# Drawing one layernorm at a time beside quantisation, and the first layernorm on VectorE, in a six-stage transformer kernel

## The chip, the cores and the metric

The kernel runs on one NeuronCore of a Trainium2 chip. The metric is device microseconds of one execution. TensorE is called PE here, VectorE DVE, ScalarE ACT, GpSimd POOL and SyncE SP, as the profile writes them.

## The reference

Sequence length 2048, width 256, 16 heads, hidden width 1024. Two kinds of feed-forward, two kinds of attention, a layernorm in front of each:

```python
x = x + 0.5 * ffn0(layernorm(x))     # stage f0: ternary-quantised weights, silu gate, rms norm
x = x + attn0(layernorm(x))          # ALiBi, causal
x = x + 0.5 * ffn0(layernorm(x))     # stage f1
x = x + 0.5 * ffn1(layernorm(x))     # stage f2: silu gate, 2:4 sparsified
x = x + attn1(layernorm(x))          # RoPE, causal
x = x + 0.5 * ffn1(layernorm(x))     # stage f3

def layernorm(x): return (x - mean(x)) / sqrt(var(x) + 1e-5)
def ternary_quant(w):                # groups of 64, in bf16
    scale = clip(mean(abs(w_g)), 1e-8); q = clip(round(w_g / scale), -1, 1); return q * scale
def ffn0(x): h = silu(x @ Wg) * (x @ Wu); return rms_norm(h) @ Wp
```

## The kernel before

Activations lie transposed: features on the 128 partitions (two halves of 256, `dc`), tokens along the free dimension, in four chunks of 512 tokens (`c` = 0 to 3). `xs[c]` holds the residual, `xns[c]` the normalised input of the next step; both are fp32 tiles of 128x2x512. The order of instructions on PE, ACT, DVE and POOL is that of the program text (a manual schedule), so Python generators decide it: each generator issues a few instructions and yields.

**A layernorm** (`layernorm(c, name)`, L244 to L278) is such a generator with about six steps. Step 1: POOL adds the two feature halves (`s`, L252). After two yields: PE sums over partitions with a matrix of 1/256 (`pm`, L256), DVE subtracts the mean (`xc`, L258), ACT squares (L261), POOL adds the halves of the squares (`v`, L263). Two yields later: PE sums `v` (`pv`, L269), `root` transposes on DVE (`tt`, L208, a single buffer) and takes the square root on ACT (L210, for which ACT loads another activation table, and a second one to go back to silu). Last step: `spread` (reciprocal L215, transpose L217 into `sd`), then two POOL products write `xn` (L274).

**Quantisation** (`quantize(i)`, L129) turns the fp32 weights of stage f0 and f1 into twelve tiles of 128x512 bf16: tiles 0 to 7 into `wgu0` (gate and up), 8 to 11 into `wp0` (down). Each has two ACT operations (L150, L152), one matmul into the single `acc` bank (`psq`, L155) and a set of six DVE operations (L158 `sc`, L162 `big`, L165 `df`, L167 `q`, L169 `wh`, L170 result). `quants` holds the generator of all of them until it is through; four sets are issued beside the first layernorm, the other eight during chunk 0 of stage f0.

**Stage f0** goes over the four chunks in order. A chunk has eight gate/up steps (`f` = 0 to 7): twelve matmuls into a pair of banks (`pg`, L311, two pairs in all, with the input as three bf16 parts), silu on ACT (`sl`, L322), product on DVE (`h`, L323), two DVE operations that split `h` into bf16 parts (`hm` L339, last part L334), and a square on ACT and a sum on POOL for the rms norm (`sq` L344, `ss` L345). At `f` = 6 or 7 the next chunk's input is split (`xm`, `xn`: L240, L241, only if its layernorm is fully issued). The tail of the chunk before (`tail0`: 24 matmuls `po` L361 for each feature half, `pss`, `tt_rms`, `y` L372, the residual update on POOL L373) is issued at `f` = 0 to 3 of the chunk after it.

What is issued beside each step comes from the deque `background`, which first holds the layernorms of chunks 1 to 3; when a chunk's tail is through, the layernorm in front of the attention (`after_f0_c`) is put behind them. `pull()` (L193) advances the first two generators of `background` by one step each; it is called once in every `f` step, right after the step's own instructions. From `f` = 4 of chunk 2 on, `go_on` also issues the start of the attention: a memset, then the key projection of chunk 0 (`pp_k`, L561, four fp32 matmul passes on `xns[0]`).

So the loop order around the change is: `f` step, quantisation, `pull()`, tail step, quantisation, split, attention start.

Of the kernel before, what the change touches and what calls it, by code (L numbers as in the profile page):

```python
# [15 lines left out]
ALU = mybir.AluOpType  # L16
# [3 lines left out]
P = 128  # L20
S = 2048
E = 256
DC = E // P
# [6 lines left out]
CH = 512  # L30
# [16 lines left out]
def macaron_kernel(ctx: ExitStack, tc: tile.TileContext, a, out):  # L47
    nc = tc.nc
# [12 lines left out]
    def ps_one(name):  # L61
        return ps3.tile([P, CH], F32, tag="one", name=name)
# [19 lines left out]
    def load_x(c, engine):  # L82
        engine.dma_start(
            out=xs[c], in_=a["xT"][:, c * CH : (c + 1) * CH].rearrange("(dc p) s -> p dc s", p=P)
        )
# [97 lines left out]
    background = deque()  # L183
# [8 lines left out]

    def pull():  # L193

        for work in list(background)[:2]:
            if next(work, "end") == "end":
                background.remove(work)

    def ready(c):

        while pending[c]:
            pull()

    def root(ps, eps, scale, name):


        tt = lpool.tile([P, CH // SLOT, SLOT], F32, tag="tt", name=f"tt_{name}")
        nc.vector.transpose(tt.rearrange("p b s -> p (b s)"), ps)  # L208
        r = lpool.tile([P, CH // SLOT], F32, tag="r", bufs=3, name=f"r_{name}")
        nc.scalar.activation(r, tt[:, :, 0], AF.Sqrt, bias=eps, scale=scale)  # L210
        return r

    def spread(r, pool, bufs, name):

        nc.vector.reciprocal(r, r)  # L215
        sd = pool.tile([P, CH], F32, tag="sd", bufs=bufs, name=f"sd_{name}")
        nc.vector.transpose(  # L217
            sd.rearrange("p (b s) -> p b s", s=SLOT),
            r.unsqueeze(2).to_broadcast([P, CH // SLOT, SLOT]),
        )  # L220
        return sd
# [19 lines left out]
        nc.vector.tensor_tensor(low(xn), mid, high(mid), ALU.subtract)  # L241
        return high(xn), high(mid), low(xn)

    def layernorm(c, name, slack=0):  # L244

        pending[c] += 1
        asked.add(name)

        def pieces():
            x, xn = xs[c], xns[c]  # L250
            s = lpool.tile([P, CH], F32, tag="s", bufs=2, name=f"s_{name}")
            nc.gpsimd.tensor_tensor(s, x[:, 0, :], x[:, 1, :], ALU.add)  # L252
            for _ in range(2 + slack):
                yield
            pm = ps_one(f"pm_{name}")
            nc.tensor.matmul(pm, lhsT=mean_m, rhs=s, start=True, stop=True)  # L256
            xc = lpool.tile([P, DC, CH], F32, tag="xc", bufs=2, name=f"xc_{name}")
            nc.vector.tensor_tensor(  # L258
                xc, x, pm.unsqueeze(1).to_broadcast([P, DC, CH]), ALU.subtract
            )  # L260
            nc.scalar.activation(xn, xc, AF.Square)  # L261
            v = lpool.tile([P, CH], F32, tag="s", bufs=2, name=f"v_{name}")
            nc.gpsimd.tensor_tensor(v, xn[:, 0, :], xn[:, 1, :], ALU.add)  # L263
            yield
            yield
            while gate[0]:
                yield
            pv = ps_one(f"pv_{name}")
            nc.tensor.matmul(pv, lhsT=mean_m, rhs=v, start=True, stop=True)  # L269
            r = root(pv, eps_ln, 1.0, f"ln_{name}")  # L270
            yield
            sd = spread(r, lpool, 2, f"ln_{name}")
            for dc in range(DC):
                nc.gpsimd.tensor_tensor(xn[:, dc, :], xc[:, dc, :], sd, ALU.mult)  # L274
            pending[c] -= 1
            yield

        return pieces()  # L278


# [181 lines left out]
    def feed_forwards(stages, beside, own=None):  # L462


        with tc.tile_pool(name=f"ffn_{stages[0][1]}", bufs=1) as hp:
# [4 lines left out]
            for s, (kind, stage, order) in enumerate(stages):  # L470
                for at, c in enumerate(order):
# [8 lines left out]
                    for f in range(FC):  # L480
                        next(work)
                        quantize_on()
                        pull()
                        if tail and f in tail[0]:
                            next(tail[1])
                            if f == tail[0][-1]:
                                tail[2]()
                                tail = None
                        draw(sparse)
                        quantize_on()  # L490
                        if kind == 0 and f >= FC - 2 and not xp and at + 1 < NCH:
                            b = order[at + 1]
                            if not pending[b]:
                                xp = split(b, own, f"{stage}_{b}")
                        beside(s, at, f)

                    def done(c=c, s=s):
                        if s == len(stages) - 1:
                            ending(c, stages[s][1])
                        else:  # L500
                            background.append(layernorm(c, f"{stages[s + 1][1]}_{c}", 1))
# [15 lines left out]
    def attention(layer, before, following):  # L517
# [9 lines left out]
        with ExitStack() as st:  # L527
# [321 lines left out]
            def output(c, dc):  # L849
                po = ps_one(f"pwo{layer}_{c}_{dc}")  # L850
                for q in range(G // 2):
                    nc.tensor.matmul(  # L852
                        po,
                        lhsT=wo[:, q, dc * P : (dc + 1) * P],
                        rhs=zs[c][:, q, :],
                        start=q == 0,
                        stop=q == G // 2 - 1,
                    )
                if layer == 0:
                    nc.vector.tensor_tensor(xs[c][:, dc, :], po, xs[c][:, dc, :], ALU.add)  # L860
                else:
                    nc.vector.scalar_tensor_tensor(
                        xs[c][:, dc, :], po, b_o[:, dc : dc + 1], xs[c][:, dc, :], ALU.add, ALU.add
                    )
                if dc == DC - 1:
                    (background if c == 0 else held).append(
                        layernorm(c, f"{following}_{c}")
                    )
# [120 lines left out]
            for i, (n, kb) in enumerate(slots):  # L989
# [40 lines left out]
                if preps and (c <= 1 or i % 2):  # L1030
                    step()
                    if c == 0 and i % 2:
                        draw(background)
                else:
                    pull()
# [8 lines left out]
    def ending(c, stage):  # L1044

        if stage == "f3":
            nc.sync.dma_start(
                out=out[:, c * CH : (c + 1) * CH].rearrange("(dc p) s -> p dc s", p=P), in_=xs[c]
            )
        else:  # L1050
            background.append(layernorm(c, f"after_{stage}_{c}", 1))

    def quantizer():

        tiles = [quantize(i) for i in range(6 * DC)]
        for i in range(3):
            next(tiles[i])
        for i, q in enumerate(tiles):
            next(q)
            if i + 3 < len(tiles):  # L1060
                next(tiles[i + 3])
            yield
            next(q)
            yield

    quants = [quantizer()]
# [37 lines left out]
        begun.clear()  # L1104

    load_x(0, nc.scalar)
    ln = layernorm(0, "f0_0")
    for k in range(6):
        next(ln)
        if k in (0, 2, 4, 5):  # L1110
# [121 lines left out]
```

## Time and profile before

| what | value |
|---|---|
| three runs | 1888.13, 1891.71, 1891.57 us; median 1891.57 |
| the profiled execution's own time | 1893.92 us |
| its span, first to last instruction | 1892.1 us, mean granted PE clock 0.973 |
| busy share of the span | PE 91%, DVE 72%, ACT 46%, POOL 21% |
| chain that ended last | PE 68%, DVE 23%, ACT 4% of the span |
| stage f0 | about 5 to 240 us of the span; its chunks begin with the first `pg` at 21, 79, 123 and 168 us |

Times in the profile are microseconds from the span's start. A row of the timeline gives start, duration, engine, line, operation, output and inputs, and in brackets the idle time of that engine before it and what ended it. A row "x2" merges two instructions in a row.

### The profile page before, as it was taken

To read this page: it belongs to the slowest core of one execution; us is meant where nothing else is said; L and a number is where in the kernel's file an instruction comes from. 1 tells how busy PE (TensorE), PEld (TensorE's weight loads), DVE (VectorE), ACT (ScalarE), POOL (GpSimd) and SP (SyncE) were. 2 spreads that over 40 slices of the span, in tenths; PEclk is the share of its full clock that TensorE was granted. 3 is DMA by queue.
4 is the path that set the end of the run, shared out by engine and by line. 5 is a ranking of instruction groups with operands and counts; after the bars stand their busy time and mean duration, and the time that the engine had idled before them with its cause. 6 is when DMAs were issued, how large, how long until landed. Compare 5 with 4: busy or idle time off the path is not lost.

```text
span 1892.1 us, 27018 instructions
## 1 busy us (share of the span) xinstructions
PE 1728.9 (91%) x10658; PEld 743.1 (39%) x10684; DVE 1359.6 (72%) x2400; ACT 878.0 (46%) x1148; POOL 406.6 (21%) x386
## 2 busy tenths in 40 slices
PE   5689988999999999798999998889999999989999
PEld 1234443433434443333434344434334344433443
DVE  7867577787788884577666667878887888816665
ACT  4234353555556667433332233445555656673221
POOL 3345620100000001345422342211011000013100
PEclk9799999999999999999999998999999999999999
DMA  4002332222211010200000134323122111000000
GB/s 133 2 1 68 111 110 66 77 56 72 89 55 47 29 29 2 75 1 0 1 12 0 39 106 128 93 80 99 53 59 85 61 36 35 11 2 0 12 12 23
DMA packets 50511, 93.11 MB, mean 49 GB/s; under 512 B 5424, under 2 KB 33072, under 8 KB 50128
## 3 DMA queue, kind: packets, MB, share of 16 engines
q1 hardware_dynamic: 49296, 89.28, 15.6%
q10 hardware_dynamic: 1088, 2.10, 0.3%
q8 instruction: 84, 1.38, 0.3%
q14 instruction: 43, 0.35, 0.1%
HBM read 59.51 MB, written 27.26 MB: 46 GB/s over the span
## 4 chain that ended last, share of the span: by engine, by line
PE 68%; DVE 23%; ACT 4%; issue 2%; POOL 1%; DMA 1%; SPq 0%; DVEq 0%; ACTq 0%; POOLq 0%
PE pav L811 14%; PE pst L776 12%; PE pq L714 11%; DVE mx L725 7%; PE pg_f L286 7%; PE pg_f L311 5%; PE po_f L297 5%; PE po_f L361 4%; PE pv L626 2%; PE pwo L852 2%; PE pp_k L561 2%; DVE h_f L334 1%; PE pp_q L561 1%; DVE hm_f L339 1%; DVE ge_f L413 1%
## 5 line engine op out<-in xcount | busy, mean ns | idle before, releaser
L725 DVE TENSOR_REDUCE mx<-pq 128x1 f32<-128x512 f32 (+3 forms) x1280 | 696.6, 601 | 137.2 <-PE pq L714 68.4
L796 ACT ACTIVATE pT<-pst 128x1024 f32<-128x1024 f32 (+3 forms) x616 | 536.0, 896 | 339.6 <-PE pst L776 177.0
L714 PE MATMUL pq<-k,q 105*128 105x512 bf16 (+7 forms) x1280 | 388.9, 353 | 49.6 <-DVE mx L725 43.6
L776 PE MATMUL pst<-q,k 99*128 99x512 bf16 (+7 forms) x1280 | 359.5, 355 | 10.5 <-ACT pT L796 6.7
L811 PE MATMUL pav<-pT,va 128*32 128x256 f32 (+1 forms) x4608 | 326.0, 379 | 6.2 <-DVE yt L832 5.0
L286 PE MATMUL pg_f<-xn,wgu 128*128 128x512 f32 x512 | 233.4, 608 | 12.5 <-DVE hr_f L323 12.5
L837 POOL TENSOR_TENSOR zt<-yt,rd 128x64 f32<-128x64 f32 x128 | 42.0, 328 | 807.6 <-DVE rd L836 807.6
L776 PEld LDWEIGHTS <-k 105*128 105x128 bf16 (+1 forms) x1280 | 111.6, 98 | 234.5 <-issue 170.2
L811 PEld LDWEIGHTS pav<-pT,va 128*32 128x32 f32 x4608 | 106.4, 109 | 189.9 <-issue 135.2
L714 PEld LDWEIGHTS <-q 105*128 105x128 bf16 (+1 forms) x1280 | 124.2, 99 | 131.9 <-issue 31.4
L311 PE MATMUL pg_f<-xn,wgu 128*128 128x512 bf16 x500 | 150.7, 406 | 20.0 <-DVE wgu L170 6.8
L322 ACT ACTIVATE sl_f<-pg_f 128x512 f32<-128x512 f32 x128 | 75.6, 591 | 190.4 <-PE pg_f L286 101.9
L286 PEld LDWEIGHTS pg_f<-xn,wgu 128*128 128x128 f32 x512 | 98.4, 194 | 143.4 <-issue 116.4
L311 PEld LDWEIGHTS <-wgu 128*128 128x128 bf16 x768 | 76.2, 99 | 163.6 <-issue 69.7
L345 POOL TENSOR_TENSOR ss_f<-ss_f,sq_f 128x512 f32<-128x512 f32 x56 | 89.8, 1604 | 142.6 <-ACT sq_f L344 131.8
L297 PE MATMUL po_f<-h_f,wd 128*128 128x512 f32 x256 | 112.7, 593 | 0.6 <-DVE h_f L441 0.6
L323 DVE TENSOR_TENSOR h_f<-sl_f,pg_f 128x512 f32<-128x512 f32 x64 | 43.6, 681 | 87.2 <-ACT sl_f L322 86.9
L722 PE MATMUL pq<-mask_qk,ident_b 128*128 128x128 bf16 x512 | 106.1, 224 | 0.0
L784 PE MATMUL pst<-mask_kq,ident_b 128*128 128x128 bf16 x512 | 102.8, 221 | 0.0
L311 PE MATMUL pg_f<-xm_f,wgu 128*128 128x512 bf16 x250 | 81.4, 406 | 16.9 <-DVE xm_f L240 16.4
L323 DVE TENSOR_TENSOR hr_f<-sl_f,pg_f 128x512 f32<-128x512 f32 x64 | 43.7, 683 | 73.8 <-ACT sl_f L322 73.4
L832 DVE STREAM_TRANSPOSE yt<-pav 128x128 f32<-128x128 f32 x128 | 39.8, 311 | 71.0 <-PE pav L811 71.0
(132 smaller groups left out, 1761.6 us busy)
## 6 DMA issues: line engine op xcount, KB each, us to landing
k<-dk SPq DMA_DIRECT2D x80, 384.0 KB
dk<-p_k SPq DMA_DIRECT2D x48, 256.0 KB
dq<-p_q SPq DMA_DIRECT2D x48, 256.0 KB
q<-dq SPq DMA_DIRECT2D x32, 384.0 KB
x<-in_xT ACTq DMA_DIRECT2D x4, 512.0 KB
raw<-in_w_gu SPq DMA_DIRECT2D x8, 256.0 KB
wgu<-in_w_gu SPq DMA_DIRECT2D x1, 2048.0 KB
cs_k<-in_cos_sin SPq DMA_DIRECT2D x4, 512.0 KB
```

The costliest lines, as they stand in the source:

```text
L286: nc.tensor.matmul(pg[:, half, :], lhsT=wgu[:, dc, half * F + f * P : half * F + (f + 1) * P], rhs=xn[:, dc, :], start=dc == 0, stop=dc == ...
L297: nc.tensor.matmul(po, lhsT=w[:, f, dc * P : (dc + 1) * P], rhs=h[:, f, :], start=f == 0, stop=f == FC - 1,)
L311: nc.tensor.matmul(pg[:, half, :], lhsT=wgu0[:, dc, half * F + f * P : half * F + (f + 1) * P], rhs=xp[part][:, dc, :], start=part == 0 an ...
L323: nc.vector.tensor_tensor(to, sl, pg[:, 1, :], ALU.mult)
L345: nc.gpsimd.tensor_tensor(ss, ss, sq, ALU.add)
L714: nc.tensor.matmul(pq, lhsT=qs[n][0:rows, hh, t * P : (t + 1) * P], rhs=ks[n, kc][0:rows, hh, 0:w], start=True, stop=kc < c,)
L722: nc.tensor.matmul(pq[:, w - P : w], lhsT=ident_b, rhs=mask_qk, start=False, stop=True)
L725: nc.vector.tensor_reduce(mxs[n][:, t, hh, kc : kc + 1], pq, AX.X, ALU.max)
L776: nc.tensor.matmul(ps[i][:, lo:CH], lhsT=ks[n, kc][0:rows, hh, t * P : (t + 1) * P], rhs=qs[n][0:rows, hh, lo:CH], start=True, stop=kc < c,)
L784: nc.tensor.matmul(ps[i][:, lo : lo + P], lhsT=ident_b, rhs=mask_kq, start=False, stop=True)
L796: nc.scalar.activation(pT[:, :, lo:CH], pair[:, :, lo:CH], AF.Exp, scale=0.25)
L811: nc.tensor.matmul(acc[hh * SLOT : (hh + 1) * SLOT, a:b], lhsT=va[kc][:, t, v0 : v0 + SLOT], rhs=pTs[hh // 2][:, hh % 2, a:b], start=kb == ...
```

## The change

`pull()` advances only the first generator of `background` as long as quantisation is not through, and the first two afterwards. And the very first layernorm (`f0_0`, which is not drawn from `background` but issued at the start) has its two sums and its product on DVE; the product becomes one instruction over 128x1024 in place of two over 128x512.

```diff
     def pull():
-        for work in list(background)[:2]:
+        for work in list(background)[: 1 if quants else 2]:
             if next(work, "end") == "end":
                 background.remove(work)
...
-    def layernorm(c, name, slack=0):
+    def layernorm(c, name, slack=0, alone=False):
...
-            nc.gpsimd.tensor_tensor(s, x[:, 0, :], x[:, 1, :], ALU.add)
+            adder = nc.vector if alone else nc.gpsimd
+            adder.tensor_tensor(s, x[:, 0, :], x[:, 1, :], ALU.add)
...
-            nc.gpsimd.tensor_tensor(v, xn[:, 0, :], xn[:, 1, :], ALU.add)
+            adder.tensor_tensor(v, xn[:, 0, :], xn[:, 1, :], ALU.add)
...
             sd = spread(r, lpool, 2, f"ln_{name}")
-            for dc in range(DC):
-                nc.gpsimd.tensor_tensor(xn[:, dc, :], xc[:, dc, :], sd, ALU.mult)
+            if alone:
+                nc.vector.tensor_tensor(
+                    xn, xc, sd.unsqueeze(1).to_broadcast([P, DC, CH]), ALU.mult
+                )
+            else:
+                for dc in range(DC):
+                    nc.gpsimd.tensor_tensor(xn[:, dc, :], xc[:, dc, :], sd, ALU.mult)
...
-    ln = layernorm(0, "f0_0")
+    ln = layernorm(0, "f0_0", alone=True)
```

## The prediction

> **What bounds the kernel now.** I read the page, then who PE waited for in the first 200 us, then the timelines of stage f0 engine by engine; the edits touch nothing else.
>
> ```profile
> PE 1728.9 (91%) x10658; PEld 743.1 (39%) x10684; DVE 1359.6 (72%) x2400; ACT 878.0 (46%) x1148; POOL 406.6 (21%) x386
> ```
>
> PE is the bound overall, but its first slices are its emptiest. The waits of PE up to 200 us (us in total, times, longest) say why: DVE.
>
> ```profile
> PE psq L155 <- DVE sc L158: 12.4, 6, 3.7
> PE pg_f L311 <- DVE xm_f L240: 7.1, 3, 2.9
> PE pg_f L311 <- DVE wgu L170: 6.8, 2, 4.7
> ```
>
> From 26.6 to 87 us DVE idles only before two `h` (4.3 and 3.1 us) and one `tt` (1.4). So chunk 0 is DVE's; from 87.43 (first `po`) on, PE runs almost without a gap. An operation of DVE with two SBUF inputs stands still until POOL's running instruction ends (DVE's timeline; POOL ran two `s_f` from 33.12 to 36.28):
>
> ```profile
> 33.62 1.50 DVE L165 TENSOR_TENSOR df<-sc,aw 128x512 bf16<-128x512 bf16 x1
> 35.05 1.50 DVE L167 TENSOR_TENSOR q<-big,sg 128x512 bf16<-128x512 bf16 x1
> 36.48 0.41 DVE L169 TENSOR_TENSOR wh<-aw,df 128x512 bf16<-128x512 bf16 x1
> ```
>
> After a long wait PE is slow too (PE's timeline):
>
> ```profile
> 123.29 0.61 PE L311 MATMUL pg_f<-xn,wgu 128*128 128x512 bf16 x2
> 126.76 1.01 PE L311 MATMUL pg_f<-xm_f,wgu 128*128 128x512 bf16 x2 [2.86 <-DVE xm_f L240]
> 128.09 1.86 PE L311 MATMUL pg_f<-xn,wgu 128*128 128x512 bf16 x4 [0.32 <-DVE xn L241]
> ```
>
> Two matmuls take 1.01, where 0.61 is usual: 0.425 us apart instead of 0.225, and the granted clock is 0.50 from 126.7 to 132.3.
>
> All times below are the profile's of before; "earlier" and "later" are against it.
>
> **The first layernorm on DVE.** POOL loses `s` (1.26), `v` (1.35) and two products (2.93). DVE gains them. No row shows a DVE sum of two fp32 SBUF halves; nearest is `hm` L339 at 0.69, the far end POOL's own 1.35; I take 0.69. The 128x1024 product lies between `xm` L240 (1.22) and POOL's 2.93; I take 1.22. A quantisation set free of POOL lasts 2.76 (63.97 to 66.73). Walk: `s` waits for the load of x (landed 5.72) and holds set 0 behind it: 5.79 to 6.48; set 0 until 9.22; `xc` as before (9.23); square until 11.53; `v`, with set 1 queued behind its 1.1 us wait, until 12.29; set 1 until 15.02 (`tt` was 15.13); `tt` and set 2 until 18.5; `sd`, product 19.5 to 20.7; set 3 until 23.46, where `xm` was 24.00, because set 3 no longer takes 4.48 beside POOL's products. **0.5 us earlier**; with the far prices 2 x 0.66 + 1.71 = 3.0 dearer, so 2.5 later.
>
> **One layernorm at a time, chunk 0.** Layernorm 2 leaves it. f=1: one `s` instead of two on POOL, so L167 takes 0.41: 1.1. f=3: one `xc` fewer (2.33 for two) and one `v` less beside set 6: 1.6. f=4 to 5: the second `tt`, which stood behind the first's square root (61.16 to 63.97), costs 2.17 less, but 1.3 of it isn't collected: the table load before `sl` of f=5 came at 64.57, behind PE's `pg`, and that `pg` can come only 3.9 earlier (3.2 collected so far, plus the `pv` passes gone in front of it); 0.9 stays. f=5: one reciprocal and `sd` (0.88) and two POOL products fewer beside set 9 (5.93, from 70.46 to 76.39, becomes 4.48): 2.3. With the first layernorm: 0.5+1.1+1.6+0.9+2.3 = **6.4 us earlier** at `xm` (81.45) and at `po` (87.43). Ends: 3.5 (POOL keeps holding DVE, phases differ) and 7.7 (the table load isn't held).
>
> **Chunk 1 takes layernorms 2 and 3, a step apart.** PE stays dense until `pg` of f=5 (with `pm` and `pv` of the second layernorm, 0.86 each, in it). What is late next is ACT and DVE: layernorm 3's root stands between `sl` of f=4 and f=5. In the trace one such root has this shape (ACT's, then POOL's timeline):
>
> ```profile
> 112.55 1.28 ACT L322 ACT_TABLE_LOAD   x1
> 113.84 0.60 ACT L322 ACTIVATE sl_f<-pg_f 128x512 f32<-128x512 f32 x1
> 117.61 2.98 POOL L274 TENSOR_TENSOR xn<-xc_f,sd_ln_f 128x512 f32<-128x512 f32 x2
> ```
>
> Layernorm 2 runs along it 0.86 later: `h` of f=4 at 115.33, `sd` 117.6, then `tt` of layernorm 3 118.3 to 119.0, root to 119.4, table load to 120.65, `sl` to 121.25, `h` of f=5 at 121.3 (was 117.34), `h` of f=6 at 124.2 (was 121.08). Then `hm`, last part and `xm` stand behind POOL's products of layernorm 3 and an `ss`, as they did behind POOL at 121.77 to 126.71 (5.6 from `h` to `xm`'s end; I count 5.9): `xm` ends at 130.1 instead of 126.7. PE waits there in both programs, so this is **3.4 us given back** (2.5 to 4); the slow clock after it was there before. The wait for `pm_after_f` at 122.33 (1.42) goes, but lies inside this one.
>
> The Trainium skill ("ScalarE: Activation LUTs", What ACT_TABLE_LOAD costs) gives a switch 1.28 us plus a drain of 1.38. The trace has the 1.28 and no drain: `sl` starts at 113.84, as the load ends. By the page, the two further switches would cost 2.8 us more, and the sum would be 7.5 instead of 4.7.
>
> **Chunk 2: the layernorm in front of the attention comes two steps later.** It now stands third behind layernorms 2 and 3. Before, its `pv` ran at 140.23 and its products early enough for `pp_k`:
>
> ```profile
> 150.34 2.52 POOL L274 TENSOR_TENSOR xn<-xc_after_f,sd_ln_after_f 128x512 f32<-128x512 f32 x2
> 158.19 1.88 PE L561 MATMUL pp_k<-xn,wqkv 128*128 128x512 f32 x4
> ```
>
> In the changed order PE has `pg` of f=3, `pv`, `pg` of f=4, `pg` of f=5, `pp_k`: `pv` adds 0.86 (its twin `pm` falls where `pv` was), and `pp_k` comes 0.86 + 2 x 2.70 = 6.3 us after `pv`'s start. What `pp_k` needs takes longer: layernorm 3 of before went through the same queue (`pv` 108.59, first product done 118.85, second 120.55), 10.3 and 12.0 us. So PE waits **4.0 us**, then for the second half. After waits of 2.9 to 4.7 us every matmul ran at 0.425 for 3.6 to 6 us: the four passes at 0.85 instead of 0.43 add 1.7, and five matmuls after them 1.0: **2.7**; with an unslowed clock the second half still costs 0.8. Sum here 0.86 + 4.0 + 2.7 = 7.6. Behind the waiting `pp_k` on PE stand all further `pg`; DVE, ACT and POOL catch up meanwhile, and from here both programs have the same order on every engine. PE's later waits up to 200 us (one of 1.71 at 186.11) hang on PE's own chain and absorb nothing. No DMA moves in its queue; SP's key stores follow `pp_k`, and the attention reads them some 50 us later.
>
> The Trainium skill ("TensorE: Matmul & The Clock Gate", Part 1) wants a whole idle window of about 3.4 us before the clock halves and gives it back after about 3.4 busy ones; the trace has it halved after 2.86. By the page, 4.0 us of idling would do, with 1.7 for the ramp instead of 2.7: a sum of 3.7.
>
> **Sum.** -6.4 + 3.4 + 7.6 = +4.6; rounded steps, so I take +4.7: 1893.92 + 4.7 = 1898.6 for an execution like the profiled one. That one lay 2.35 above the median; on the median, 1891.57 + 4.7 = 1896.3.
>
> **Rivals.** (A) Not slower: the two later waits are covered. If POOL's first product comes within 6.3 us of `pv` and `xm` isn't held, only the early gain and the 0.86 remain: -5.5, 1886.1. For it: each term of the gain is a stall that a row shows; against it: 10.3 us measured for that very path. It decides from 6.3 us down. (B) The waits come, the first shorter, and the clock is not slowed: -6.4 + 2.5 + 0.86 + 4.0 + 0.8 = +1.8, 1893.4. For it: 1.42 and 2.07 us waits left the clock alone; against: 2.86 did not. (C) The early gain is not there: POOL's remaining work meets DVE elsewhere, or DVE's sums take POOL's prices: -3.5 + 3.4 + 7.6 = +7.5, 1899.1; with 2.5 lost at the start as well, +10. That the change doesn't do what it says is excluded by the order of the changed program: layernorm 2's first `pm` stands in chunk 1.
>
> **How the numbers follow.** Forecast 0.57, A 0.10, B 0.18, C 0.15. A measurement of this kernel can tell about 0.2%, 3.8 us, from no change (its runs span 3.6). Faster by more: A, 0.10. Within: B and a fifth of the forecast's spread, 0.30. Slower: 0.60. The range leaves out A and the upper half of C: -1.6 to +8.0, 1890.0 to 1899.6.
>
> **What would show it.** Right: `xm` of chunk 1 near 75, first `po` near 81; a PE wait for `xm` of chunk 2 of over 4 us; a PE wait of about 4 us for POOL's `xn` before the first `pp_k`, with a granted clock near 0.5 behind it; the rest of the timeline shifted by a constant. Wrong: no wait before `pp_k`, or a first `po` not earlier than 84.

## The result, and the profile after

The changed kernel took 1897.68 us (median of 20 runs), the kernel before 1891.74 us (20 runs beside them): ratio over all runs 1.0029 (of the medians alone 1.0031), 95% interval 1.0023 to 1.0035; by the medians it is 5.9 us slower where 4.7 were forecast. A later measurement gave 1.0051 (1.0037 to 1.0065, 5 runs of after), so the loss is settled, but its size only to some 4 us (the two ratios stand for 5.5 and 9.6 us). The profiled execution of after has a span of 1898.1 us, 6.0 longer than before's 1892.1, and a mean granted clock of PE of 0.974 of full speed (before 0.973). Line numbers from L254 on are 2 to 7 higher than before, most by 7 (`xm` is still L240, `pg` L318, `po` L368, `pp_k` L568).

The page's busy line of after: DVE has three more operations (two sums of 0.69 and the wide product of 1.22), yet its total fell by 3.2 us; the rows of chunk 0 below show operations that are no longer stretched beside POOL.

```profile
PE 1726.3 (91%) x10658; PEld 742.9 (39%) x10684; DVE 1356.4 (71%) x2403; ACT 883.2 (47%) x1152; POOL 402.0 (21%) x382
```

Who PE waited for in the first 200 us of after (us in total, times, longest):

```profile
PE psq L155 <- DVE sc L158: 12.8, 5, 3.4
PE pg_f L318 <- DVE xm_f L240: 10.4, 3, 4.7
PE pg_f L318 <- DVE wgu L170: 6.2, 2, 4.7
...
PE pp_k L568 <- POOL xn L281: 4.2, 2, 3.9
PE pg_f L318 <- DVE h_f L330: 3.8, 2, 3.0
```

The `xm` line grew from 7.1 to 10.4, the one of `h` (in chunk 1) from 0.2 to 3.8, and `pp_k` waiting for POOL is new. Chunk 0, on DVE's timeline, shows what the change was meant to remove; only one `s` of a layernorm is beside this set, so one operation is stretched where two were:

```profile
32.84 1.51 DVE L165 TENSOR_TENSOR df<-sc,aw 128x512 bf16<-128x512 bf16 x1
34.28 0.41 DVE L167 TENSOR_TENSOR q<-big,sg 128x512 bf16<-128x512 bf16 x1
34.61 0.41 DVE L169 TENSOR_TENSOR wh<-aw,df 128x512 bf16<-128x512 bf16 x1
```

PE's timeline at the three places that the forecast rests on (the first `po`, `xm` of chunk 2, the first `pp_k`):

```profile
80.13 0.52 PE L368 MATMUL po_f<-h_f,wp 128*128 128x512 bf16 x1
...
123.90 1.01 PE L318 MATMUL pg_f<-xm_f,wgu 128*128 128x512 bf16 x2 [4.69 <-DVE xm_f L240]
126.17 1.86 PE L318 MATMUL pg_f<-xn,wgu 128*128 128x512 bf16 x4 [1.26 <-DVE xn L241]
...
161.51 1.30 PE L568 MATMUL pp_k<-xn,wqkv 128*128 128x512 f32 x2 [3.88 <-POOL xn L281]
163.18 2.08 PE L568 MATMUL pp_k<-xn,wqkv 128*128 128x512 f32 x2 [0.37 <-POOL xn L281]
```

Read against before, the distance between the two programs runs like this (negative: after is earlier). First `po`: 80.13 for 87.43, -7.30. `xm` of chunk 2: 123.90 for 126.76, -2.86. The `pg` after that chunk's `po`: 135.95 for 137.53, -1.58. First `pp_k`: 161.51 for 158.19, +3.32. Its next `pg`: 165.05 for 159.91, +5.14, and the one after: +5.47. From there the distance stays the same up to 208 us: the first `pv` of the attention, my milestone in what follows, stands at 191.59 for 186.11, +5.48. (Over the whole span it is 6.0.) So 7.3 us were gained in chunk 0, 5.7 given back around chunk 2's start, 4.9 lost before `pp_k` and 2.15 behind it: -7.3 + 5.7 + 4.9 + 2.15 = +5.45.

### The profile page after: what moved, and what is told of

Its sections match the earlier page's. It is cut to its first block, busy times and chain, and to the rows that moved or that the text cites. A ratio compares the mean times of both kernels' runs of the same rounds, so it can differ in the third digit from the quotient of the medians.

```text
span 1898.1 us, 27014 instructions
## 1 busy us (share of the span) xinstructions
PE 1726.3 (91%) x10658; PEld 742.9 (39%) x10684; DVE 1356.4 (71%) x2403; ACT 883.2 (47%) x1152; POOL 402.0 (21%) x382
## 4 chain that ended last, share of the span: by engine, by line
PE 66%; DVE 24%; ACT 5%; issue 2%; DMA 1%; POOL 1%; SPq 0%; ACTq 0%; DVEq 0%; POOLq 0%
PE pav L818 14%; PE pst L783 12%; PE pq L721 10%; DVE mx L732 8%; PE pg_f L293 6%; PE pg_f L318 5%; PE po_f L304 5%; PE po_f L368 4%; DVE h_f L341 2%; PE pv L633 2%; PE pp_k L568 2%; PE pwo L859 2%; PE pp_q L568 1%; DVE ge_f L420 1%; DVE hm_f L346 1%
## 5 line engine op out<-in xcount | busy, mean ns | idle before, releaser
L318 PE MATMUL pg_f<-xn,wgu 128*128 128x512 bf16 x498 | 150.0, 406 | 22.1 <-DVE h_f L330 6.7
L318 PEld LDWEIGHTS <-wgu 128*128 128x128 bf16 x768 | 76.2, 99 | 169.9 <-issue 76.1
L318 PE MATMUL pg_f<-xm_f,wgu 128*128 128x512 bf16 x252 | 82.5, 409 | 20.0 <-DVE xm_f L240 19.6
```

The source lines that it names most:

```text
L318: nc.tensor.matmul(pg[:, half, :], lhsT=wgu0[:, dc, half * F + f * P : half * F + (f + 1) * P], rhs=xp[part][:, dc, :], start=part == 0 an ...
```

## The experiments

Theory: the change is one gain (chunk 0) and two later waits, both from layernorms that are now drawn later; the first layernorm on DVE is nearly neutral. Rivals are told with each run. Each ratio is to the kernel before, measured beside it. One profiled execution can differ by 2 to 4 us from the median of its kernel (the last section has a likely cause), so the ratio says how much, and the trace where.

| kernel | ratio (95%) | `xm` of chunk 2 | first `pp_k` | first `pv` against before |
|---|---|---|---|---|
| before | 1 | 126.76 | 158.19 | 0 |
| after | 1.0029 (1.0023 to 1.0035) | 123.90 | 161.51 | +5.5 |
| after, again | 1.0051 (1.0037 to 1.0065) | 123.12 | 160.61 | +4.5 |
| e1: first layernorm on DVE only | 0.9992 (0.9982 to 1.0001) | 125.09 | 155.93 | -2.3 |
| e2: one at a time only | 1.0036 (1.0023 to 1.0049) | 124.10 | 161.64 | +5.6 |
| e3: after, three drawn | 0.9985 (0.9974 to 0.9996) | 123.38 | 153.81 | -4.4 |
| e4: after, PE busy before `pp_k` | 1.0027 (1.0017 to 1.0037) | 123.74 | 161.36 | +4.1 |
| e5: after, chunk 2's layernorm alone | 1.0021 (1.0012 to 1.0030) | 118.37 | 157.69 | +1.3 |
| e6: after, chunk 3's layernorm last | 1.0000 (0.9991 to 1.0009) | 119.07 | 152.68 | +0.1 |
| e7: before, `after_f0_0` two steps later | 1.0037 (1.0024 to 1.0049) | 125.98 | 162.10 | +5.8 |
| e8: after, PE busy before chunk 2's `xm` | 1.0018 (1.0009 to 1.0027) | 126.67 | 159.93 | +3.5 |
| e9: as e6, then all three | 1.0002 (0.9993 to 1.0011) | 120.31 | 154.90 | -2.2 |
| e10: e9 with PE busy twice | 1.0035 (1.0022 to 1.0048) | 125.50 | 162.85 | +5.8 |
| e12: e3 with PE busy before chunk 2's `xm` | 0.9980 (0.9966 to 0.9994) | 123.80 | 153.04 | -5.2 |

**The two halves of the change.** e1 keeps the first layernorm on DVE and undoes the drawing:

```diff
-        for work in list(background)[: 1 if quants else 2]:
+        for work in list(background)[:2]:
```

> Only one half of the change: the first layernorm's sums and product are on VectorE, and two layernorms at a time are drawn from, as in the kernel before. Theory (the drawing makes nearly all of the difference): the first xm comes 0.7 us earlier, as in the trace of after, and nothing else moves, so 1891.7 - 0.7 = 1891.0 us, ratio to before 0.9996; h of f=1 to f=5 0.7 earlier and no more, the wait of TensorE for xm of chunk 2 near the 2.9 us of before, none for xn before the first pp_k. Rival (the first layernorm's move to VectorE pushes later work and makes the loss): 1897 us or so, with the 3.9 us wait before pp_k.

e2 keeps the drawing and puts the first layernorm back on POOL:

```diff
-    ln = layernorm(0, "f0_0", alone=True)
+    ln = layernorm(0, "f0_0")
```

> Only the other half: one layernorm at a time beside quantisation, the first layernorm on GpSimd as before. Theory: after's 1897.7 plus the 0.7 us that the first layernorm on VectorE had saved: 1898.4 us, ratio to before 1.0035; first po some 6.6 us earlier than in before, the wait for xm of chunk 2 near 4.7 us and the wait before the first pp_k near 3.9 us, as in after. Rival (the first layernorm's move makes the loss): 1885 to 1892 us, without those waits.

e1 was not slower (0.9992), with no wait before `pp_k` and one of 2.86 us for `xm` of chunk 2, before's length; e2 took the whole loss (1.0036), with a wait of 4.68 us for `xm` of chunk 2 and of 3.88 before `pp_k`, the same as in after. The rival, that moving the first layernorm makes the loss, is out. In e1's trace the first `xm` comes 0.6 earlier, as expected; its `pp_k` is 2.3 earlier, more than expected, because PE's slow stretches were shorter: 6.8 us where before had 10.2 behind chunk 1's `xm`, 3.4 where it had 6.8 behind chunk 2's.

**The wait before `pp_k`: taken away, and made alone.** e3 draws three layernorms once quantisation is over, which puts the matmuls of `after_f0_0` back where before had them; e7 takes the kernel before and holds the same layernorm two steps longer, so that it stands where after has it, without any gain in chunk 0.

```diff
# e3, on after
-        for work in list(background)[: 1 if quants else 2]:
+        for work in list(background)[: 1 if quants else 3]:
# e7, on before
-            background.append(layernorm(c, f"after_{stage}_{c}", 1))
+            slack = 3 if (stage, c) == ("f0", 0) else 1
+            background.append(layernorm(c, f"after_{stage}_{c}", slack))
```

> After, but once quantisation is over three layernorms are drawn from instead of two, so that the layernorm behind chunk 0 (after_f0_0) is drawn together with those of chunks 2 and 3 and its matmuls stand where they stood in before. Theory: the wait before the first pp_k goes, with the slow matmuls behind it: 4.9 + 0.6 us, so 1897.7 - 5.5 = 1892.2 us; pm_after back in the last steps of chunk 1 gives TensorE a wait there again (1.4 us in before), so 1892 to 1894, ratio 1.0003 to 1.0012. Rival (the wait before pp_k only covers a wait that comes later anyway, at pp_q or pv, and the loss comes from chunk 2's xm): 1896 to 1899 us.

> Before, with the layernorm behind chunk 0 (after_f0_0) held two steps longer before its first matmul, so that its matmuls stand where they stand in after; nothing else is changed, no early gain. Theory: the wait before the first pp_k appears, 4 us, with 1.4 to 2.2 us behind it and 0.9 of moved passes: 1891.4 + 6 = 1897.4 us, ratio 1.0032. Rival (that wait comes only because chunks 1 and 2 run differently in after): no wait before pp_k, 1890 to 1892 us.

PE's timeline in e3 has no wait at `pp_k`; in e7 it has the same one as after, to the hundredth:

```profile
153.81 1.88 PE L568 MATMUL pp_k<-xn,wqkv 128*128 128x512 f32 x4
```

```profile
151.80 1.02 PE L269 MATMUL pv_after_f<-v_after_f,mean_m 128*128 128x512 f32 x2
...
162.10 3.74 PE L561 MATMUL pp_k<-xn,wqkv 128*128 128x512 f32 x4 [3.88 <-POOL xn L274]
```

In e7, 10.3 us pass from `pv_after` to `pp_k`, as from 151.21 to 161.51 in after. The late layernorm by itself costs 0.37% (7.0 us, interval 4.5 to 9.3) where the theory had 6: shown. Taking it away gained more than I expected, 0.9985 where 1.0003 to 1.0012 stood in the expectation: e3 is faster than before. Of the 9.9 us that e3 has over after at the `pg` behind the second `pp_k` (159.94 for 169.80), 0.5 lie before the first `po`, 1.3 at chunk 2's start, 5.9 between there and `pp_k`, and 2.2 behind; the 5.9 hold the wait of 3.9, the 0.86 of `pm`, which moved out of that stretch, and 1.0 of after's slow clock, which reached 2.1 us past its first `po` there (129.54 to 131.6).

**What the 2.15 us behind the wait are.** e4 gives PE idle work during the wait:

```diff
+                if layer == 0 and what == "k" and c == 0:
+                    spare = ps_acc("spare")
+                    for _ in range(16):
+                        nc.tensor.matmul(spare, lhsT=half_m, rhs=wgu0[:, 0, 0:CH], start=True, stop=True)
```

> After, with 16 idle bf16 matmuls of 128x512 into a spare PSUM bank just before the first pp_k (nothing reads them): some 16 x 0.225 = 3.6 us, so that TensorE is busy in its wait of 3.9 us for xn. Theory (the matmuls behind the wait are slow because TensorE stood idle): the granted clock stays at 1 behind it, the 2.2 us of slow matmuls go, 1897.7 - 2.2 = 1895.5 us, ratio 1.0020. Rival (the slow stretch has another cause, such as the float32 matmuls of pp_k themselves): no gain, 1897.7 us, or up to 0.5 us more where the idle matmuls end after xn has come.

PE's timeline in e4, from the idle matmuls to the second `pp_k`:

```profile
157.30 3.61 PE L568 MATMUL spare<-wgu,half_m 128*128 128x512 bf16 x16
161.36 1.12 PE L574 MATMUL pp_k<-xn,wqkv 128*128 128x512 f32 x2 [0.45 <-POOL xn L281]
163.03 1.12 PE L574 MATMUL pp_k<-xn,wqkv 128*128 128x512 f32 x2 [0.55 <-POOL xn L281]
...
166.70 1.88 PE L574 MATMUL pp_k<-xn,wqkv 128*128 128x512 f32 x4
```

The granted clock stays at 1 and the passes are fast; `xn` comes when it came. From `pp_k` to `pp_k` it is 5.34 us here, 6.58 in after and 4.43 in before. So the slow clock is 6.58 - 5.34 = 1.2 us, and 0.9 is POOL's second product, which comes 1.67 us after the first where two passes last 0.86. The expectation gave all 2.2 to the clock. The ratio (1.0027) can't tell 1.2 us from nothing; the trace can.

**Why chunk 2's `xm` came late.** e5 draws the layernorm of chunk 2 alone until it is through, then two; e6 lets `after_f0_0` in as soon as it exists and keeps chunk 3's for last; e9 is e6 with all three drawn from then on. `through`, which these lines use, is a set into which each layernorm puts its name when its last step is issued.

```diff
# e5
-        for work in list(background)[: 1 if quants else 2]:
+        for work in list(background)[: 1 if quants or "f0_2" not in through else 2]:
# e6 (e9: 3 in place of 2)
+        alone = quants or len(background) == 2 and "f0_2" not in through
+        for work in list(background)[: 1 if alone else 2]:
...
+            at = 1 if (stage, c) == ("f0", 0) else len(background)
+            background.insert(at, layernorm(c, f"after_{stage}_{c}", 1))
```

> After, but drawing stays at one layernorm at a time until the layernorm of chunk 2 is through; only then are that of chunk 3 and the one behind chunk 0 drawn, together, the latter where it stands in after. Theory (xm of chunk 2 is late in after because layernorm 3's root and products stand beside chunk 1): TensorE's waits for h in chunk 1 (0.8 and 3.0 us) go and xm of chunk 2 comes some 3.5 us earlier, near 120.5; the wait of 3.9 us before the first pp_k stays: 1897.7 - 3.5 = 1894.2 us, ratio to before 1.0015. Rival (xm of chunk 2 is held by GpSimd's sums s_after and ss alone, whatever layernorm 3 does): xm stays within 1 us of 123.9, 1897 us or more.

> After, with the layernorm of chunk 2 alone until the one behind chunk 0 (after_f0_0) comes, then these two, and that of chunk 3 last. The matmuls of after_f0_0 stand where they stood in before. Theory (the early part of chunk 0 is a gain of 7 us that two later waits eat): both waits go and the gain stays, first pp_k near 151, 1891.4 - 7 = 1884.4 us, ratio 0.9963; between 1883 and 1887. Rival (layernorm 3, now beside chunk 2, makes a new wait of its own there, 3 to 5 us, as layernorm 2 did beside chunk 1 in after): 1888 to 1890 us, not under the kernel that draws three.

> After, with the layernorm of chunk 2 alone until the one behind chunk 0 (after_f0_0) comes, and then all three together: the matmuls of chunk 3's layernorm stand one step earlier than in the kernel that drew it last, before those of after_f0_0. Theory (a layernorm costs where its products and sums on GpSimd stand beside xm): xm of chunk 2 near 119, no wait before pp_k, and xm of chunk 3 in time again, so that first pv of the attention comes near 181, 5 us earlier than in before: ratio 0.997 to 0.9985, 1886 to 1889 us where before is 1892. Rival (three layernorms over two chunks cost the same wherever the third stands): ratio 1.000, 1892 us.

In e5 `xm` of chunk 2 comes at 118.37, 5.5 us earlier than in after, and the waits for `h` (0.8 and 3.0) shrink to one of 0.2. POOL's `s_after` still runs beside the split, as in after, so the rival is out: layernorm 3's root and products were what held chunk 1 (PE's timeline, then POOL's, of e5).

```profile
115.60 1.13 PE L259 MATMUL pm_f<-s_f,mean_m 128*128 128x512 f32 x2 [3.08 <-POOL s_f L255]
...
118.37 1.01 PE L320 MATMUL pg_f<-xm_f,wgu 128*128 128x512 bf16 x2 [1.00 <-DVE xm_f L241]
```

```profile
117.20 2.24 POOL L255 TENSOR_TENSOR s_after_f<-x 128x512 f32<-128x512 f32 x1
```

PE now waits 3.1 us in front of `xm` for POOL's `s` of layernorm 3, a wait that after does not have. The rest of the expectation holds too: the wait before `pp_k` stays (3.87). But the ratio, 1.0021, lies only 0.08% under after's first one and inside its reach; that the 4.2 us seen at `pv` are a gain in time is not shown.

e6 removes the wait before `pp_k` and brings the one for `xm` of chunk 2 back to 2.85 us, before's length, with `pp_k` at 152.68, 5.5 us earlier than in before, and then loses all of it: 1.0000, the rival's case, a little slower even than it stated. The place is the next chunk boundary, where layernorm 3 now stands (PE's timeline of e6):

```profile
164.13 0.61 PE L321 MATMUL pg_f<-xm_f,wgu 128*128 128x512 bf16 x2 [1.14 <-DVE xm_f L242]
166.41 1.87 PE L321 MATMUL pg_f<-xn,wgu 128*128 128x512 bf16 x4 [1.67 <-DVE xn L243]
```

POOL's products of layernorm 3 push its later sums back by some 3 us, so that one of them runs beside the split of chunk 3 on DVE, and a slow stretch of 6.8 us follows (165.6 to 172.4). e9 repairs that boundary (waits of 0.4 and 0.7) and pays elsewhere: PE stands 5.86 us before `xm` of chunk 2 for POOL's `s` of layernorm 3. Its ratio, 1.0002, is the rival's: moving the third layernorm about only moves its price. e3, which leaves layernorms 2 and 3 side by side in chunk 1, did better than e9; their intervals just overlap, and the cause is not settled.

**Keeping PE busy elsewhere.** e8 puts 20 such idle matmuls between the first two and the next matmuls of chunk 2, on after. e10 puts 12 there and 12 at the same place of chunk 1, on e9. e12 puts 16 at chunk 2, on e3.

```diff
+                if name == "f0_2_0" and half == 0 and part == 1:
+                    spare = ps_acc("spare")
+                    for _ in range(20):
+                        nc.tensor.matmul(spare, lhsT=half_m, rhs=wgu0[:, 0, 0:CH], start=True, stop=True)
```

> After, with 20 idle bf16 matmuls of 128x512 into a spare PSUM bank (nothing reads them) in TensorE's wait of 4.7 us for xm of chunk 2, between its first two and its next matmuls. Theory (the clock is halved for whole periods of some 3.4 us after a period in which TensorE was mostly idle): no halved clock between 118 and 135, the matmuls from xm to the second project of chunk 1 gain 2 to 3 us, 1897.7 - 2.3 = 1895.4 us, ratio 1.0020. Rival (the matmuls there are slow for want of their operands): no gain, 1897.7 us.

> The kernel of the run before it in this call, with 12 idle bf16 matmuls of 128x512 (2.7 us, read by nothing) in each of TensorE's waits for xm of chunk 1 and of chunk 2. Theory (a wait of about 3 us often halves the clock for the next period of 3.4 us or two, in which dense matmuls lose half): 1.5 us less at each of the two places, ratio 0.0015 below that kernel's, 1884 to 1886 us where before is 1892. Rival (the halved periods come as often as before, because the waits in front of psq in chunk 0 set them): no difference.

> The kernel that draws three layernorms after quantisation (the fastest so far, ratio 0.9985), with 16 idle bf16 matmuls of 128x512 (3.6 us, read by nothing) in TensorE's wait of 4.1 us for xm of chunk 2, as in the run that kept TensorE busy there in after. Theory (both measures are independent: the wait before pp_k stays away, and the clock is not halved behind xm of chunk 2): ratio 0.9975 to 0.9985, no wait before pp_k, no halved clock between 118 and 132. Rival (drawing three was faster only by the phase of the halved periods in its runs, and on another chip gains nothing): ratio 1.000 or more.

e8: 1.0018 where 1.0020 was expected, but the trace is mixed. Behind the idle matmuls the clock stays at 1 up to `pp_k`; in front of them it was halved from 115.5 to 122.3, from within the wait of 3.0 us for `h` on, so PE reached them late and they ended after `xm` was there. e10 went wrong by its own edit: the spare bank is the one that `psq` uses, and in chunk 1 PE stood in front of the idle matmuls until the quantiser had read it:

```profile
79.47 5.16 PE L323 MATMUL spare<-wgu,half_m 128*128 128x512 bf16 x12 [6.05 <-DVE sc L158]
```

It says nothing on the theory. e12 did as the theory said: no wait before `pp_k`, no halved clock between 80.0 and 230, ratio 0.9980 (0.9966 to 0.9994). It is the fastest kernel here, on another chip than e3's. That speaks against the rival (a lucky phase), but e3 without the idle matmuls was not run on that chip, so the rival is not ruled out for e3 itself; that e12 beats e3 lies within their intervals.

**After once more**, beside e9 and e10:

> After once more, unchanged, beside the same runs of before as the two others of this call: ratio 1.0029 again, 1897.5 us where before is 1892. If its profiled run has other periods of halved clock than the first one (121.4 to 131.6 then), the edges lie on another grid of 3.41 us, and first pv comes up to 3 us earlier or later than 191.6.

Ratio 1.0051, more than expected. Its slow stretches were 120.3 to 130.5 and 161.3 to 164.7 (the first time 121.4 to 131.6 and 162.3 to 165.8), and its first `pv` came at 190.61, 1.0 earlier. Why these five runs lay 0.2% further from before than the first twenty stays open.

## Why the prediction was right

Direction, place and size held: slower, through the two waits that it named, 1897.68 us against 1896.3 and inside 1890.0 to 1899.6. By its steps:

- **Chunk 0, -6.4:** measured -7.3. The steps up to `h` of f=3 came out near their sizes (3.54 in all, 3.2 forecast). The mis-sized one is f=4 to 5: I held back 1.3 us because the silu table load would stand behind PE's `pg`; in after it starts at 59.77, right behind the square root (59.43, 0.32 long), and `h` of f=5 comes 5.04 earlier where 4.1 were forecast (ACT's timeline of after). The first layernorm on DVE gave 0.7 (forecast 0.5), at the prices taken: both sums 0.69, the product 1.22.

```profile
59.77 1.28 ACT L329 ACT_TABLE_LOAD   x1
61.06 0.60 ACT L329 ACTIVATE sl_f<-pg_f 128x512 f32<-128x512 f32 x1
```

- **Chunk 2's `xm`, +3.4 given back:** measured +5.7, beyond its upper end of 4. The mechanism was the one named, layernorm 3's root between two `sl` and POOL's products beside the split, and e5 shows it. The size failed in two collisions on DVE that the walk left out. At f=3 of chunk 1, `hm` and the last part took 1.10 and 1.81 where 0.69 and 0.75 are usual, beside POOL's residual update and `ss`, and so `tt` of layernorm 2 came 1.1 later than walked and `xm` 1.0. And the second half of the split ran beside POOL's `s_after` (DVE's timeline, then POOL's, of after):

```profile
103.43 1.10 DVE L346 TENSOR_TENSOR hm_f<-h_f 128x512 f32<-128x512 f32 x1
104.45 1.81 DVE L341 TENSOR_TENSOR h_f<-hm_f 128x512 bf16<-128x512 f32 x1
...
121.57 2.27 DVE L240 TENSOR_TENSOR xm_f<-xn 128x1024 f32<-128x1024 f32 x1
123.88 2.24 DVE L241 TENSOR_TENSOR xn<-xm_f 128x1024 bf16<-128x1024 f32 x1
```

```profile
122.72 2.24 POOL L254 TENSOR_TENSOR s_after_f<-x 128x512 f32<-128x512 f32 x1
```

  L241 took 1.30 in before: 0.9 more. The last 0.3 is the slow clock, which the forecast took as the same in both programs: it ran 2.1 us past the chunk's first `po` in after and 1.3 in before (the forecast read it there as 126.7 to 132.3, the trace has 126.0 to 132.8). The forecast dealt with `s_after` only through PE's wait for `pm_after`; it looked at who waits for POOL's result and not at which DVE operation stands beside it.
- **Before `pp_k`, 0.86 + 4.0:** measured 4.90, with a wait of 3.88. The 10.3 us read from layernorm 3's path in before was the path's length in after, 10.3; rival A needed 6.3.
- **Behind it, +2.7:** measured 2.15, of which e4 gives 1.2 to the clock and 0.9 to the second product. The forecast charged the slow passes in full and took the length of the slow stretch from other waits (3.6 to 6 us); here it was 3.4.
- **Sum:** the errors -0.9, +2.3 and -0.55 make +0.85, and 4.6 + 0.85 = 5.45. The closeness of the total owes something to errors of both signs.
- **Rivals:** A is out (both waits came); B is out, as the clock was slowed at both places; C is out, as the early gain came, larger than forecast. The table loads cost 1.28 each: in chunk 1, where the two roots now stand apart, `sl` starts at 108.52 and 114.37, as the loads of 107.23 and 113.08 end, so the drain that the forecast weighed beside them does not show here either.

## What to carry to other kernels

Thinning the work beside a stage that is bound by another engine gains there, but the work comes back as somebody's input later. Follow each delayed generator to its consumer and compare two lengths, its own path (10.3 us here) and the time that the consumer's queue leaves it (6.3). A change like this should take away the cause in the crowded stage and restore the old order behind it, as e3 does with one number. And for each step that is moved, look at what runs beside it on the other engine, not only at who waits for its result.

## What the runs showed of the hardware

The clock of PE is halved and restored at points of a fixed grid, not a set time after a wait. In before's profile up to 215 us the granted clock changes at 40.6, 44.0, 54.3, 61.1, 71.4, 74.8, 78.2, 88.4, 126.0 and 132.8: every distance is a multiple of 3.413 us within 0.1, the step of the reading (126.0 - 40.6 = 25 x 3.41, 132.8 - 126.0 = 2 x 3.41). After changes at 49.7, 56.5, 73.6, 80.4, 121.4, 131.6, 162.3 and 165.8, again 3.41 apart or multiples of it, with another start. All fourteen profiles fit such a grid up to 245 us, each with its own phase, which is why the same wait is followed by 3.4, 6.8 or 10.2 us at half speed. Divided along the grid, the stretches of before around chunk 2's start read (us, length, PE busy and matmuls, granted clock, DMA share, GB/s):

```profile
119.20:122.60 3.40, 1.99 (x9) 1.00 0.00 0
122.60:126.00 3.40, 1.30 (x4) 1.00 0.00 0
126.00:129.40 3.40, 2.32 (x6) 0.50 0.00 0
129.40:132.80 3.40, 3.40 (x10) 0.50 0.00 0
132.80:136.20 3.40, 3.40 (x16) 1.00 0.00 0
```

A stretch in which PE was busy for 1.30 of 3.4 us is followed by half speed, one with 1.99 is not; 2.32 does not end the half speed, 3.40 does. Divided like this from 27 to 215 us, all fourteen profiles say the same: the clock fell only after stretches with at most 1.55 us of work, and stayed only after 1.39 or more (between the two it did either); it came back only after 2.70 or more and never after 2.56 or less. The prediction's 2.86 us wait that halved the clock, and the shorter ones that didn't, fit this: what counts is the work within one stretch of the grid.

The granted clock reads 1.00 before its first recorded change, and that is not to be trusted. In before two matmuls at 29.12 take 1.05 us, two at 30.86 take 0.61, the first the half speed and the second the full one, while the reading is 1.00 at both; the switch between them, near 30.4, is a point of the same grid (three steps of 3.41 before 40.6).

The Trainium skill ("TensorE: Matmul & The Clock Gate", Part 1) describes a free-running window of 4096 cycles at 1.2 GHz, 3413 ns, which does not restart with the kernel. The edges above agree with it. Its table asks for an idle window before the clock halves; if that means a window without work, the row with 1.30 us of work in it differs, and the measurement decides. In the prediction I had read the page as a fixed idle time and left the free-running part out.

A price of one slow stretch taken from one execution is therefore a draw: with 1 to 3 stretches of 3.41 us, each at half speed, the same wait costs up to 1.7, 3.4 or 5.1 us (an estimate, half of 3.41 for each). That fits runs of one kernel that spread over 2 to 11 us (before: 1886.70 to 1894.59), though this was not separated from other causes of spread.
